# Attention over short heads, fused with two feed-forward layers and a second attention: a new order of halvings, row sums, reciprocal and quotient within a group, and one addition for both units of squares of 32

## The chip, the cores and the metric

The kernel runs on one core of one Trainium2 chip. The metric is the time of one execution on the device in microseconds (us), as the median of several runs. Besides that there is one execution that the hardware profiler recorded; every busy time, wait and start time below is from that one.

## The reference, cut to what matters

The input x has 8 batches of 512 tokens with 256 channels. Four layers are added to it one after the other: attention A, a feed-forward layer, attention B, and the same feed-forward layer again. The change touches attention A only. It does not attend over tokens. Each token is projected to 16 heads of 64 channels, and within one token and head every query channel attends to the key channels up to its own:

```python
scores = jnp.einsum('bshq,bshk->bshqk', Q, K)          # an outer product of 64 x 64 per token and head
mask = jnp.triu(jnp.ones((C, C), dtype=bool), 1)
scores = jnp.where(mask, -jnp.inf, scores)
w = jax.nn.softmax(scores, axis=-1)
attn = jnp.einsum('bshqk,bshk->bshq', w, V)
x = x + attn.reshape(b, s, HID) @ Wo + bo
```

So per token and head there is a lower triangle of 64 x 64 exponentials, its row sums (the denominators) and the row sums of exponentials times v (the numerators).

## The kernel before, in words

**Groups and units.** Attention A is cut into 128 groups: 8 batches, 4 groups of 4 heads each, 4 tiles of 128 tokens. In a group the 128 tokens lie on the partitions. The triangle of each head is cut into its diagonal and squares below it: one square of 32, two of 16, four of 8 and so on down to 32 of 1. The squares are worked off in four units, written here u0 to u3:

```python
units = (((32, 0, 2),), ((16, 0, 4),), ((32, 2, 2),), ((8, 0, 4), (4, 0, 4), (2, 0, 4), (1, 0, 4)))
```

Unit u0 has the squares of 32 of heads 0 and 1, u2 those of heads 2 and 3, u1 all squares of 16, u3 the small ones. A unit passes through these stages:

- `scores` (L784): products of queries and keys, by POOL for u0 and u2 in two halves and by DVE for u1 and u3. For u0 DVE also makes the diagonal (L771).
- `exps` (L798, L793): exponentials on ACT.
- `weigh` (L808, L805): exponentials times v on DVE, written beside the exponentials.
- `halve` (L814): for u0, u1 and u2, a DMA issued by POOL adds the second half of the tile onto the first (1 MB, an accumulating transfer).
- `fold` (L819): for u0 and u2, POOL adds two halves of what is left.
- `gather` (L845): row sums on DVE into small tiles `red`.
- `add_rows` (L852): POOL adds the tiles `red` to `acc`, which holds the denominators and numerators of the group.
- `small_squares` (L835, L852): POOL adds the squares of 2 and 1 of u3 to `acc` without a row sum.
- `invert` (L856), `divide` (L860): the reciprocal of the denominators on DVE, the quotient on POOL.
- `turn_group`, `project_out`, `new_x`: transposes and the output projection on PE, copies on ACT.

**Order.** The instructions of PE, DVE, ACT and POOL are issued in the order in which the program writes them down; only the loads on SP's queue are ordered by the build. `AttentionA.step(n)` writes one step of a software pipeline. Step n starts unit n (`scores`), makes the exponentials of unit n-1, weighs and halves unit n-2, and takes later stages of earlier units; `self.at(n - k)` is the unit of k steps ago. A step has three parts, ended by `yield`. Four steps make one group. After each part the main loop lets the generator `after_a` (feed-forward layers and attention B of the batches that attention A has done) write as much as a fixed pace allows; that starts at step 75. `later_weights` (`prep`) is a second generator that prepares weights for later layers and bounds for the scores at the start; one piece of it is written after every part from step 2 on. `fit_qkv(g)` fits the projection weights of head group g to the layer norm: g = 0 on DVE ahead of the loop, g = 1, 2, 3 on POOL after steps 0, 1, 2. `measure(b)` makes the layer-norm statistics of batch b ten steps ahead of its first unit.

**Buffers.** `w` (u0 and u2) has three buffers, `acc` three. Row sums of squares of 32 have two buffers `red64`, all others three buffers `red128`.

Of the kernel before, what the change touches and what calls it, by code (L numbers as in the profile page):

```python
# [9 lines left out]
F32 = mybir.dt.float32  # L10
# [3 lines left out]
ALU = mybir.AluOpType  # L14
AX = mybir.AxisListType

P = 128
# [9 lines left out]
GW = GH * C  # L27
NG = HID // GW
# [256 lines left out]
def fast_path(ctx: ExitStack, tc: tile.TileContext, k, t, flag):  # L285

    nc = tc.nc
# [123 lines left out]
    def later_weights():  # L411

        braw = block("braw")[0:3].rearrange("p (n f) -> p n f", n=4)
        part16 = block("part16", BF16)[0:3, : 2 * D]
        for j, row in enumerate((t.bo, t.b_bp)):
            nc.sync.dma_start(braw[:, 0, j * D : (j + 1) * D], row.broadcast_to([3, D]))
        yield
        for j in range(3):  # L420
            nc.scalar.copy(part16, braw[:, 0])
            nc.scalar.copy(braw[:, 2], part16)
            nc.gpsimd.tensor_tensor(braw[:, 0], braw[:, 0], braw[:, 2], ALU.subtract)
            yield
            if j == 0:
                nc.vector.tensor_scalar_mul(braw[:, 3], braw[:, 2], ident[0:3, 0:1])
            else:
                nc.vector.scalar_tensor_tensor(
                    braw[:, 3], braw[:, 2], ident[0:3, j : j + 1], braw[:, 3], ALU.mult, ALU.add
                )  # L430
        yield
        nc.scalar.copy(bias16.rearrange("p j f -> p (j f)"), braw[:, 3])

        wbqk = block("wbqk").rearrange("p (c f) -> p c f", c=DC)
        rows = block("rows")
        w3 = block("w3").rearrange("p (c f) -> p c f", c=MC)
        wbvp = block("wbvp")[:, : 2 * DC * D].rearrange("p (j c f) -> p j c f", j=2, c=DC)
        n_qk = 2 * BG * P
        s3 = rows[:, n_qk + D : n_qk + 2 * D]
        nc.sync.dma_start(s3, t.s3.broadcast_to([P, D]))  # L440
        nc.sync.dma_start(w3, t.w3.rearrange("(c p) f -> p c f", p=P))
        nc.sync.dma_start(wbqk, t.w_bqk.rearrange("(c p) j f -> p c (j f)", p=P))
        nc.sync.dma_start(wbvp[:, 0], t.w_bv.rearrange("(c p) f -> p c f", p=P))
        nc.sync.dma_start(wbvp[:, 1], t.w_bp.rearrange("(c p) f -> p c f", p=P))
        nc.sync.dma_start(
            rows[:, :n_qk], t.w_bqk[D - 1 : D].rearrange("o j f -> o (j f)").broadcast_to([P, n_qk])
        )
        nc.sync.dma_start(rows[:, n_qk : n_qk + D], t.w_bv[D - 1 : D].broadcast_to([P, D]))
        yield
        for c in range(MC):  # L450
            nc.gpsimd.tensor_tensor(w3[:, c, :], w3[:, c, :], s3, ALU.mult)
            if c % 2:
                yield
        for w, row, cols in ((wbqk, t.b_bqk_row, slice(0, n_qk)), (wbvp[:, 0], t.b_bv, slice(n_qk, n_qk + D))):
            for c in range(DC):
                nc.gpsimd.tensor_tensor(w[:, c], w[:, c], rows[:, cols], ALU.subtract)
                yield
            nc.sync.dma_start(w[P - 1 : P, DC - 1, :], row)

        nc.sync.dma_start(w3_d, w3.rearrange("p c f -> p (c f)"))  # L460
        nc.sync.dma_start(wbqk_d, wbqk.rearrange("p c f -> p (c f)"))
        nc.sync.dma_start(wbvp_d, wbvp.rearrange("p j c f -> p (j c f)"))
        yield
        yield from bound_scores()
# [139 lines left out]
    class AttentionA:  # L604
# [32 lines left out]

        def step(self, n):

            weighed = self.at(n - 2)  # L640
            if weighed[0] is not None:
                self.weigh(*weighed)
            unit = self.at(n)
            on_pool = unit[3] in (0, 2)
            if on_pool:
                half = self.scores(*unit)
                next(half)
            if weighed[0] is not None:
                self.halve(*weighed)
            if on_pool:  # L650
                next(half, None)
            b, i, g, u = self.at(n + 40)
            if u == 0 and g == 0 and i == 0 and b > 0:
                self.x[b] = load_x(b)
            b, i, g, u = self.at(n + 10)
            if u == 0 and g == 0 and i == 0:
                self.measure(b)
            b, i, g, u = self.at(n + 8)
            if u == 0 and g == 0:
                self.live["xn"] = normed(self.x[b][:, i, :], *self.rn[b, i], "a")  # L660
            b, i, g, u = self.at(n - 5)
            if u == NU - 1:
                self.invert(b, i, g)
            b, i, g, u = self.at(n - 4)
            if u == 1:
                self.gather(b, i, g, u)
            b, i, g, u = self.at(n + 7)
            if u == 0 and g == 0:
                nc.scalar.copy(self.live[b, i], self.live.pop("ps_ln"))
            if self.at(n - 1)[0] is not None:  # L670
                self.exps(*self.at(n - 1))
            yield
            if unit[0] is not None and not on_pool:
                for _ in self.scores(*unit):
                    pass
            for args in self.sums:
                self.add_rows(*args)
            self.sums = []
            b, i, g, u = self.at(n - 5)
            if u == NU - 1:  # L680
                self.divide(b, i, g)
            b, i, g, u = self.at(n - 2)
            if u == NU - 1:
                self.small_squares(b, i, g)

            b, i, g, u = self.at(n - 4)
            if u == 0:
                self.fold(b, i, g, u)
            b, i, g, u = self.at(n - 3)
            if u == 2:  # L690
                self.fold(b, i, g, u)
            b, i, g, u = self.at(n - 9)
            if u == NU - 1:
                self.new_x(b, i, g)
            b, i, g, u = self.at(n + 2)
            if u == 0:
                self.keep_qk(b, i, g)
            b, i, g, u = self.at(n - 7)
            if u == NU - 1:
                self.turn_group(b, i, g)  # L700
            b, i, g, u = self.at(n - 8)
            if u == NU - 1:
                self.project_out(b, i, g)
            b, i, g, u = self.at(n + 3)
            if u == 0:
                self.project(b, i, g)
            yield
            b, i, g, u = self.at(n - 4)
            if u == 2:
                self.gather(b, i, g, u)  # L710
            b, i, g, u = self.at(n - 5)
            if u == 0:
                self.gather(b, i, g, u)
            b, i, g, u = self.at(n - 3)
            if u == NU - 1:
                self.gather(b, i, g, u)
            b, i, g, u = self.at(n - 7)
            if u == NU - 1:
                nc.scalar.copy(self.live["att"], self.live.pop("pta"))
            b, i, g, u = self.at(n + 8)  # L720
            if u == 0 and g == 0:
                self.live[b, i] = lnp.tile([P, DC, P], F32, tag="xnt_a", name=f"xnta_{b}_{i}", bufs=NT)
                self.live["ps_ln"] = turned_over(self.live.pop("xn"), half_bank().rearrange("p (c s) -> p c s", c=DC))
            yield
# [113 lines left out]
        def gather(self, b, i, g, n_u):  # L838


            w = self.live.pop((b, i, g, n_u))
            for n, off, nsq, cols in squares(units[n_u]):
                if n > 2:
                    red = ap_.tile([P, 2, nsq * n], F32, tag=f"red{nsq * n}", name=f"red_{b}_{i}_{g}_{n_u}_{n}", bufs=2 + (n < 32))
                    nc.vector.tensor_reduce(red, self.columns_of(w, n, off, nsq), AX.X, ALU.add)  # L845
                    self.sums.append((b, i, g, n, cols, red))

        def add_rows(self, b, i, g, n, cols, part):

# [491 lines left out]
    with tc.manual_schedule(engines={ET.PE, ET.DVE, ET.Activation, ET.Pool}):  # L1341
        a = AttentionA()
        prep = later_weights()
        fit_qkv(0)
        weights = None
        done, spent = after_a(), 0
        for n in range(-10, a.steps):
            for part, _ in enumerate(a.step(n)):
                if n >= 2:
                    next(prep, None)  # L1350
                while 3 * spent * each < total * (3 * (n - each - 11) + part + 1):
                    spent += next(done)
            if 0 <= n < NG - 1:
                fit_qkv(n + 1)
        for _ in done:
            pass
    judge()
# [86 lines left out]
```

## Time and profile before

| | |
|---|---|
| median of 3 runs | 4010.42 us (4006.96 to 4017.54) |
| the profiled execution | 4009.55 us, span 4007.6 us |
| PE busy | 2958.0 us (74%) |
| DVE busy | 3376.7 us (84%) |
| ACT busy | 2337.2 us (58%) |
| POOL busy | 3098.1 us (77%) |
| transfers of q0, POOL's queue | 570.46 MB, 62.9% of 16 engines' span |
| granted TensorE clock, mean | 0.845 |

The span runs from the first to the last instruction; the profiled execution takes 2 us more. Four stretches differ in kind. Up to about 200 us the pipeline fills and weights are prepared. From 201 to 509 us attention A runs alone, 13 groups. From 580 to 3653 us feed-forward layers and attention B of earlier batches are woven in, 107 groups. From 3653 us on only the last batch's later layers are left, and PE is busy for 322 of 355 us. In a group of rows "busy, mean ns" is the time of the whole group and of one instruction; consecutive instructions of one engine overlap by up to 0.1 us, or by up to 0.3 us on POOL, so a chain is summed from start to next start. A DMA on POOL's queue holds POOL for some 0.6 us and lands later.

### The profile page before, as it was taken

Reading aid. Unit: us, or ns where it says so; the run is one execution under the profiler, and the core shown is the slowest. Engines: PE = TensorE matmul, PEld = TensorE weight load, DVE = VectorE, ACT = ScalarE, POOL = GpSimd, SP = SyncE. Lnnn points to the kernel's source line nnn. Section 1 sums busy time; section 2 is a strip of 40 time slices with the busy share of each in tenths; the row PEclk is TensorE's granted clock in tenths of the full one; section 3 lists DMA queues with packets and bytes.
Section 4 is the critical chain, followed back from the end, with each engine's and each line's share of the span. In section 5 each row is a group of like instructions: output and inputs, shape, how many; then the busy total and the mean of one; then the engine's idle time right before and its main releaser. Section 6 shows DMA issues by size and latency. Waiting matters only on the chain.

```text
span 4007.6 us, 37678 instructions
## 1 busy us (share of the span) xinstructions
PE 2958.0 (74%) x12328; PEld 2012.2 (50%) x12328; DVE 3376.7 (84%) x3777; ACT 2337.2 (58%) x3145; POOL 3098.1 (77%) x3051
## 2 busy tenths in 40 slices
PE   1543478777876888768787788768787778768988
PEld 0311145355653656346553566346653556436847
DVE  4899988998889888998989988998889988897115
ACT  2433465666755766666755767567656667555342
POOL 6688888887888887887888888888888878886211
PEclk7555689888987989889897889879898899879999
DMA  8566777668776777668776688668877687767304
GB/s 240 114 141 145 146 182 182 147 161 199 199 162 126 195 188 196 150 147 210 174 192 139 168 198 214 147 131 198 195 181 151 154 199 205 155 133 210 126 29 167
DMA packets 118653, 671.07 MB, mean 167 GB/s; under 512 B 12704, under 2 KB 31915, under 8 KB 43824
## 3 DMA queue, kind: packets, MB, share of 16 engines
q0 software_dynamic: 78336, 570.46, 62.9%
q1 hardware_dynamic: 40112, 98.11, 6.8%
q8 instruction: 100, 1.64, 0.2%
q14 instruction: 105, 0.86, 0.1%
HBM read 255.90 MB, written 9.96 MB: 66 GB/s over the span
## 4 chain that ended last, share of the span: by engine, by line
DVE 38%; PE 16%; POOL 14%; DMA 12%; issue 8%; ACT 8%; POOLq 0%; DVEq 0%; ACTq 0%
DVE red L845 15%; DMA w<-w 12%; DVE w L808 10%; PE ph L1120 5%; ACT w L798 3%; POOL w L819 3%; DVE ws L808 3%; POOL w L784 3%; PE pqkb L1167 3%; DVE ws L784 3%; POOL acc L852 3%; DVE w L784 2%; POOL w L814 2%; DVE acc L856 2%; POOL h L1036 2%
## 5 line engine op out<-in xcount | busy, mean ns | idle before, releaser
L798 ACT ACTIVATE w<-w 128x2048 f32<-128x2048 f32 x384 | 734.2, 1913 | 653.8 <-POOL w L784 440.8
L1120 PE MATMUL ph<-h,hidden 128*128 128x512 f32 x4096 | 1047.9, 412 | 77.4 <-POOL h L1036 45.5
L784 POOL TENSOR_TENSOR w<-k 128x1024 f32<-128x1024 f32 x512 | 1076.2, 2102 | 9.6 <-ACT k L762 9.0
L1120 PEld LDWEIGHTS ph<-h,hidden 128*128 128x128 f32 x4096 | 795.3, 196 | 282.1 <-POOL h L1036 55.9
L808 DVE TENSOR_TENSOR w<-w,qv 128x1024 f32<-128x1024 f32 x768 | 899.8, 1213 | 22.4 <-ACT w L798 22.3
L845 DVE TENSOR_REDUCE red<-w 128x128 f32<-128x1024 f32 (+1 forms) x384 | 601.8, 1567 | 171.6 <-DMA w<-w 94.6
L819 POOL TENSOR_TENSOR w<-w 128x1024 f32<-128x1024 f32 x256 | 643.1, 2512 | 72.5 <-DMA w<-w 71.9
L814 POOL DMA_DIRECT2D w<-w x384 | 337.1, 878 | 339.7 <-issue 134.8
L852 POOL TENSOR_TENSOR acc<-acc,red 128x256 f32<-128x256 f32 (+1 forms) x640 | 471.0, 736 | 152.3 <-DVE red L845 124.5
L845 DVE TENSOR_REDUCE red<-ws 128x256 f32<-128x2048 f32 (+1 forms) x256 | 435.5, 1743 | 0.0
L746 PE MATMUL qv<-wqv,xnta 128*128 128x512 f32 x512 | 299.3, 715 | 89.9 <-DVE ws L808 82.4
L808 DVE TENSOR_TENSOR ws<-ws,qv 128x1024 f32<-128x1024 f32 (+3 forms) x512 | 294.7, 638 | 49.4 <-ACT ws L798 49.4
L1052 PE MATMUL pw<-xnt,gate 128*128 128x512 f32 (+2 forms) x1152 | 298.8, 419 | 24.9 <-ACT silu L1028 18.0
L784 DVE TENSOR_TENSOR w<-qv,k 128x1024 f32<-128x1024 f32 x256 | 301.3, 1219 | 3.6
L784 DVE TENSOR_TENSOR ws<-qv,k 128x1024 f32<-128x1024 f32 (+3 forms) x512 | 299.8, 648 | 0.0
L868 PE MATMUL bank<-ident,acc 128*128 128x128 f32 x256 | 64.3, 341 | 287.5 <-ACT k L761 287.1
L798 ACT ACTIVATE ws<-ws 128x1920 f32<-128x1920 f32 x128 | 231.5, 1809 | 75.3 <-DVE ws L784 74.7
L1052 PEld LDWEIGHTS pw<-xnt,gate 128*128 128x128 f32 x1152 | 227.6, 213 | 82.1 <-ACT silu L1028 22.3
L1229 ACT ACTIVATE eb<-psb 128x256 f32<-128x256 f32 (+3 forms) x512 | 182.2, 443 | 146.6 <-PE psb L1226 146.3
L1146 PE MATMUL pof<-w,h 128*128 128x256 f32 x1024 | 247.9, 396 | 19.4 <-ACT h L1085 19.4
L1085 ACT ACTIVATE h<-ph,s_sb 128x512 fp32r<-128x512 f32 (+1 forms) x256 | 171.1, 688 | 145.9 <-PE ph L1120 144.6
L856 DVE RECIPROCAL acc<-acc 128x256 f32<-128x256 f32 x128 | 223.2, 1744 | 12.3 <-POOL acc L852 12.3
(143 smaller groups left out, 4723.5 us busy)
## 6 DMA issues: line engine op xcount, KB each, us to landing
w<-w POOLq DMA_DIRECT2D x384, 1024.0 KB, 7.7
hidden<-in_h POOLq DMA_DIRECT2D x128, 1024.0 KB, 7.9
gate<-in_w12p POOLq DMA_DIRECT2D x32, 1024.0 KB, 9.0
w<-w_d SPq DMA_DIRECT2D x16, 1024.0 KB, 12.0
wqv<-wqv_d SPq DMA_DIRECT2D x31, 512.0 KB
wo<-in_wo SPq DMA_DIRECT2D x32, 256.0 KB, 7.4
wbqk<-wbqk_d SPq DMA_DIRECT2D x8, 1024.0 KB
w<-in_h SPq DMA_DIRECT2D x8, 1024.0 KB, 7.0
```

The lines of the kernel that those rows point to most:

```text
L746: nc.tensor.matmul(qv.rearrange("p j f -> p (j f)"), xnt[:, c, :], wqv[:, c, :], start=(c == 0), stop=(c == DC - 1),)
L784: eng.tensor_tensor(e, rows(q).to_broadcast(shape), columns(kt[:, 0]).to_broadcast(shape), ALU.mult)
L798: nc.scalar.activation(e, e, AF.Exp, scale=C**-0.5)
L808: nc.vector.tensor_tensor(ev, e, columns(qv[:, 1]).to_broadcast(list(e.shape)), ALU.mult)
L814: nc.gpsimd.dma_start(w[:, :2048], w[:, 2048:], accum_op=ALU.add)
L819: nc.gpsimd.tensor_tensor(w[:, :1024], w[:, :1024], w[:, 1024:2048], ALU.add)
L845: nc.vector.tensor_reduce(red, self.columns_of(w, n, off, nsq), AX.X, ALU.add)
L852: nc.gpsimd.tensor_tensor(rows, rows, part.rearrange("p a (x i) -> p a x i", i=n), ALU.add)
L856: nc.vector.reciprocal(acc[:, 0, :], acc[:, 0, :])
L1052: nc.tensor.matmul(pj[:, toks], w[:, m % 4, j, c, :], xs[:, p, c, toks], start=(p == 0 and c == 0), stop=(p == 1 and c == DC - 1),)
L1120: nc.tensor.matmul(pss[j], w[:, j, c, :], h_in(p, c), start=(p == 0 and c == 0), stop=(p == 1 and c == MC - 1),)
L1146: nc.tensor.matmul(po, h(0, c)[:, i * P : (i + 1) * P], w3[:, c, :], start=(c == 0), stop=False)
```

## The change

- The fold of u0 moves from step n-4, second part, to step n-3, first part, ahead of POOL's scores and of the halving of u1.
- The row sum of u1 stays in its step but moves ahead of `weigh`. The row sum of u0 moves from n-5 to n-4, that of u2 from n-4 to n-5, both in the third part. The row sums of u3 stay.
- The reciprocal moves from n-5 to n-6, to the very start of the step; the quotient from n-5 to n-6, second part, behind the fold of u2.
- The row sums of u0 and u2 go into the two halves of one tile `red1`, and one addition per group takes both. All other row sums use `red0`. Both have two buffers.
- `measure(0)` is written ahead of `fit_qkv(0)`. `prep` advances once a step, from step 3 on. `fit_qkv(1)`, `(2)`, `(3)` come after steps 4, 14 and 24.

```diff
         def step(self, n):
+            b, i, g, u = self.at(n - 6)
+            if u == NU - 1:
+                self.invert(b, i, g)
+            b, i, g, u = self.at(n - 4)
+            if u == 1:
+                self.gather(b, i, g, u)
             weighed = self.at(n - 2)
             if weighed[0] is not None:
                 self.weigh(*weighed)
+            b, i, g, u = self.at(n - 3)
+            if u == 0:
+                self.fold(b, i, g, u)
             unit = self.at(n)
...
             if u == 0 and g == 0 and i == 0:
-                self.measure(b)
+                if b > 0:
+                    self.measure(b)
...
-            b, i, g, u = self.at(n - 5)
-            if u == NU - 1:
-                self.invert(b, i, g)
-            b, i, g, u = self.at(n - 4)
-            if u == 1:
-                self.gather(b, i, g, u)
...
             self.sums = []
-            b, i, g, u = self.at(n - 5)
-            if u == NU - 1:
-                self.divide(b, i, g)
             b, i, g, u = self.at(n - 2)
             if u == NU - 1:
                 self.small_squares(b, i, g)
 
-            b, i, g, u = self.at(n - 4)
-            if u == 0:
-                self.fold(b, i, g, u)
             b, i, g, u = self.at(n - 3)
             if u == 2:
                 self.fold(b, i, g, u)
+            b, i, g, u = self.at(n - 6)
+            if u == NU - 1:
+                self.divide(b, i, g)
...
             yield
             b, i, g, u = self.at(n - 4)
-            if u == 2:
+            if u == 0:
                 self.gather(b, i, g, u)
             b, i, g, u = self.at(n - 5)
-            if u == 0:
+            if u == 2:
                 self.gather(b, i, g, u)
...
                 if n > 2:
-                    red = ap_.tile([P, 2, nsq * n], F32, tag=f"red{nsq * n}", name=f"red_{b}_{i}_{g}_{n_u}_{n}", bufs=2 + (n < 32))
-                    nc.vector.tensor_reduce(red, self.columns_of(w, n, off, nsq), AX.X, ALU.add)
-                    self.sums.append((b, i, g, n, cols, red))
+                    if n_u != 2:
+                        self.live["red", n] = ap_.tile(
+                            [P, 2, GW // 2], F32, tag=f"red{n // 32}", name=f"red{n}_{b}_{i}_{g}"
+                        )
+                    red = self.live["red", n]
+                    part = red[:, :, cols.start // 2 : cols.stop // 2]
+                    nc.vector.tensor_reduce(part, self.columns_of(w, n, off, nsq), AX.X, ALU.add)
+                    if n_u != 0:
+                        self.sums.append((b, i, g, n, slice(0, GW), red))
...
         a = AttentionA()
         prep = later_weights()
+        a.measure(0)
         fit_qkv(0)
...
-                if n >= 2:
+                if n >= 3 and part == 2:
                     next(prep, None)
...
-            if 0 <= n < NG - 1:
-                fit_qkv(n + 1)
+            if n in (4, 14, 24):
+                fit_qkv(n // 10 + 1)
```

## The prediction

> **What bounds the kernel now.** I began with the busy time by stretch, because the shares of the whole span mix three stages. Attention A alone runs from 201 to 509 us, attention A with the feed-forward work woven in from 580 to 3653 us, and the last batch's remainder from there to the end.
>
> ```profile
> 201.00:509.00 308.00, 124.20 (x215) 58.67 (x215) 307.42 (x319) 119.97 (x122) 269.00 (x238) 0.55 0.70 146
> 580.00:3653.00 3073.00, 2393.12 (x10211) 1635.39 (x10210) 2768.40 (x3107) 1975.45 (x2653) 2558.38 (x2512) 0.87 0.74 173
> ```
>
> The columns are PE, PEld, DVE, ACT, POOL. In the first stretch DVE is busy 307.42 of 308 us: it is the bound and waits for nothing. The reciprocal runs once a group and 13 times there, so a group costs 308/13 = 23.7 us. In the second it runs 107 times: 3073/107 = 28.7 us a group, with DVE busy 25.9 and POOL 23.9. DVE has 2.8 us of gaps in each group. The waits of DVE there, then the landing of the halvings (L814) in the two stretches:
>
> ```profile
> DVE red L845 <- DMA w<-w: 84.0, 37, 4.9
> DVE red L845 <- POOL w L819: 72.2, 27, 5.6
> DVE acc L856 <- POOL acc L852: 11.4, 10, 2.2
> ```
> ```profile
> DMA to landing us min/median/max: 6.9/7.1/8.0
> ```
> ```profile
> DMA to landing us min/median/max: 6.9/7.8/16.7
> ```
>
> So 156 us are lost ahead of row sums. No halving ever lands in less than 6.9 us. Last, the timeline of one group without feed-forward work, DVE and then POOL:
>
> ```profile
> 331.17 1.74 DVE L856 RECIPROCAL acc<-acc 128x256 f32<-128x256 f32 x1
> 332.83 2.28 DVE L808 TENSOR_TENSOR ws<-ws,qv 128x1024 f32<-128x1024 f32 x4
> 335.03 2.28 DVE L845 TENSOR_REDUCE red<-w 128x256 f32<-128x2048 f32 x1
> 337.34 2.36 DVE L784 TENSOR_TENSOR w<-qv,k 128x1024 f32<-128x1024 f32 x2
> ```
> ```profile
> 326.93 0.87 POOL L814 DMA_DIRECT2D w<-w  x1 [2.65 <-issue]
> 327.54 2.35 POOL L852 TENSOR_TENSOR acc<-acc,red 128x128 f32<-128x128 f32 x3
> 329.86 1.95 POOL L784 TENSOR_TENSOR w<-k 128x1024 f32<-128x1024 f32 x1
> 331.75 0.85 POOL L814 DMA_DIRECT2D w<-w  x1
> 332.36 2.23 POOL L784 TENSOR_TENSOR w<-k 128x1024 f32<-128x1024 f32 x1
> 334.28 0.98 POOL L860 TENSOR_TENSOR acc<-acc 128x256 f32<-128x256 f32 x1
> 334.96 2.60 POOL L819 TENSOR_TENSOR w<-w 128x1024 f32<-128x1024 f32 x1
> 337.45 0.79 POOL L852 TENSOR_TENSOR acc<-acc,red 128x256 f32<-128x256 f32 x1
> 338.14 0.67 POOL L835 TENSOR_TENSOR ws<-ws 128x256 f32<-128x256 f32 x1
> 338.89 1.66 POOL L852 TENSOR_TENSOR acc<-acc,ws 128x256 f32<-128x256 f32 x2
> 340.50 2.36 POOL L819 TENSOR_TENSOR w<-w 128x1024 f32<-128x1024 f32 x1
> 342.83 1.96 POOL L784 TENSOR_TENSOR w<-k 128x1024 f32<-128x1024 f32 x1
> 344.73 0.85 POOL L814 DMA_DIRECT2D w<-w  x1
> ```
>
> Both engines keep the program's order. What matters is distance: before, several other instructions stand between each halving and its reader, and between the last sums (327.54) and the small squares (338.14).
>
> **What the Trainium skill says.** "DMA: Bandwidth & Descriptors", section SWDGE vs HWDGE vs iDMA: an accumulating transfer can be issued from GpSimd only. The trace agrees, all 384 stand in POOL's queue, so each waits behind what POOL was given earlier. The same page, Anatomy of one DMA: a transfer's semaphore wait happens on the issuing sequencer before dispatch; and its fit, 2.0 us plus bytes over 436 thousand, gives an estimate of 4.4 us for 1 MB. The trace differs, 6.9 at the least, and decides. "Trainium Architecture — The Big Picture", Inside one NeuronCore: engines run in parallel and meet only at semaphores. The trace agrees: the 2.65 us of POOL at 326.93 end with DVE's product.
>
> **The change part by part.** I number a group's steps r0 to r3 (step n modulo 4) and its units u0 to u3. After the change POOL's order is: r0 scores of u0 (first half), halving of u2, scores of u0 (second half), *one* addition for both squares of 32; r1 addition of 16, small squares, fold of u2, quotient; r2 scores of u2 (first half), halving of u0, second half; r3 fold of u0, halving of u1, two additions. DVE in r1 is: reciprocal, row sum of u1, products of u3, scores of u1.
>
> Two new waits come of it. First, the fold of u0 stood in r0 behind three other steps' work and now follows its halving with only half a score between (1.92 us): POOL must wait for the landing, and the halving of u1 is queued behind that wait. Second, u2's row sum moves to the end of r3, so the addition of 32 comes after r0's scores on POOL; the reciprocal is DVE's very next work and waits for it, and behind the reciprocal are queued the row sum of u1 and the products of u3, for which POOL's small squares wait. POOL waits for DVE and DVE for POOL, in turn.
>
> This closes a chain that comes back to its own start one group later. From start to next start in the timeline above: reciprocal 1.66, row sum of u1 2.31, products of u3 2.28 (together 6.25 on DVE); small squares with their additions 2.36, fold of u2 2.33, quotient 0.69, half a score 1.90 (7.28 on POOL); landing of u0 at the least 6.9 and its hand-over 0.07 (6.97); fold of u0 2.37, issue of u1's halving 0.61, two additions 1.39, half a score 1.90, issue of u2's halving 0.61, half a score 1.92, addition of 32 0.73 (9.53); hand-overs 0.1. The sum is 30.1 us, against 23.7. The same method on the order of before (row sum of u1, addition, small squares, fold, scores, addition, halving of u1, landing) gives 19.8, under DVE's 23.7, as the full DVE shows.
>
> With feed-forward work: the median landing is 0.7 longer (7.8 for 7.1). POOL's feed-forward work between 580 and 3653 us (L1036 144, L934 102, L529 to L532 107) is 353/107 = 3.3 us a group; of twelve places where it is put, six lie on the chain (the others fall into POOL's two waits): 1.65. I add 0.5 for late landings of u2 and waits of that work: 33.0 us a group, 4.3 more than 28.7. Bounds: 30.5, if all of it hides and landings are short; 34.5, if it all lies on the chain.
>
> The rest is small. One addition fewer a group saves 128 x 0.69 = 88 us of POOL's time, counted in the chain already. Moving batch 0's statistics ahead of fitting g = 0: the row sum of x waits until 14.65 us behind the fit, though x is there at 3; the projection still needs the fitted weights, so I take 3 us of 22 (bounds 0 and 7). Preparation once a step and the three later fits: before, ACT stood 21.9 us for the load of `sk` and DVE 24.7 behind it; groups 0 to 5 took 165 us (36 to 201). After: 5 x 30.1 plus half of the preparation's 16 us of POOL (L423 4.3, L451 5.5, L456 6.6; half of its places are on the chain), 159. Its SP loads now have two steps to land; I keep 5 us for what stays (0 to 15). The fits lie in POOL's waits: nothing, 11 us at most if that cover is gone. Together about -4. One buffer fewer for `red` costs nothing: POOL has read each before its turn to be filled comes again. The end after 3653 is bound by PE (322 of 355 us busy): unchanged.
>
> Sum: -4 + 13 x 6.4 (83) + 107 x 4.3 (460) = +539. The two groups between 509 and 580 are left equal. On the profiled execution's 4009.55 us (span 4007.6, 2 around it; the median of the runs, 4010.42, is 1 away) that is **4550 us**.
>
> **The rivals.** *Only the transfers bind*: the reciprocal finds its sums ready, for instance because POOL runs ahead. The chain is then row sum 2.31, products 2.28, POOL 7.28, landing 6.97, fold 2.37, landing of u1 6.9: 28.1 alone; with two landings longer by 0.7, two of twelve places (0.55) and the 0.5 above, 30.6: 13 x 4.4 + 107 x 1.9 - 4 = +256, 4266 us. For it speaks that today's reciprocal waits only 11.4 us in all; against it, that the addition is now later than the scores in POOL's order.
>
> *Faster*: DVE stays the bound, and the 156 us ahead of row sums go, since folds and sums of u2 stand a step further apart, and some 25 us at the start: about 3830 if all, 3900 if half the former comes back as other waits. It decides from the point where the chain is under 28.7 us a group. My sum is above it by 4.3, and by 1.4 even alone with the shortest landings; a mis-read order of one queue would be needed.
>
> *The change doesn't do what it says*: the order is not kept by the engines, and the time is 4010. The trace of before shows the written order on both, so this is small.
>
> **How the numbers follow.** Main case 0.72, transfers only 0.19, faster 0.06, no change 0.03. The main case alone reaches from 4250 (30.5 us a group) to 4660 (34.5); the second lies inside. So 4250 to 4650 leaves out the 0.09 of the other two and the ends. About 0.3%, 12 us, is what a measurement of this kernel can tell from no change. Slower 0.92, same 0.02, faster 0.06.
>
> **What would show it.** Right: groups of about 30 us before the feed-forward starts, DVE busy there near 78% and no longer full; the reciprocal waiting some 5 us for POOL's addition in most groups; POOL's fold waiting some 4 us for the landing of u0; the halving of u1 issued over 9 us after that of u0, where it was 5.9 (from 321.02 to 326.93). Wrong: a group still at 23.7 us in that stretch, or a reciprocal that doesn't wait (then the second case), or row sums of u1 that wait for the transfer.

## The result and the profile after

The median of 4 runs is 4628.45 us (4626.05 to 4630.83), against 4008.69 us (4004.39 to 4017.54) for the kernel before on the same chip: 1.1543 times as long, with a 95% interval from 1.1521 to 1.1564. The profiled execution took 4626.84 us, its span is 4625.0 us. That is 617 us more than the profiled execution before. First the engines' busy time over the whole span, and its share of the span:

```profile
PE 3042.5 (66%) x12328; PEld 2037.5 (44%) x12328; DVE 3381.9 (73%) x3777; ACT 2341.9 (51%) x3145; POOL 3074.4 (66%) x2923
```

DVE is busy for 3381.9 us, as before (3376.7), but that is now 73% of the span where it was 84%. The same two stretches as in the prediction show where the rest went. The columns are again PE, PEld, DVE, ACT, POOL, and then the granted TensorE clock, the busy share of the DMA engines and their GB/s; 13 reciprocals, so 13 groups, fall in the first stretch and 107 in the second:

```profile
193.00:592.00 399.00, 140.86 (x314) 78.13 (x313) 314.14 (x328) 124.90 (x129) 273.75 (x228) 0.53 0.55 114
672.00:4262.00 3590.00, 2475.56 (x10218) 1658.59 (x10216) 2768.94 (x3107) 1980.86 (x2655) 2537.86 (x2404) 0.83 0.64 148
```

Alone, a group takes 399/13 = 30.7 us (23.7 before) and DVE is busy 79% of it; it is no longer the bound. With feed-forward work it takes 3590/107 = 33.55 us (28.7 before). DVE's work in 107 groups is what it was (2768.94 us, 2768.40 before), so all that was added there is idle time. Over the whole span, the waits at three places before, and then DVE's and POOL's main waits after, are these; an entry gives the waiting engine and line, what it waited for, the total in us, how often, and the longest:

```profile
DVE acc L856 <- POOL acc L852: 12.3, 11, 2.2
DVE red L845 <- DMA w<-w: 94.6, 39, 7.2
POOL w L819 <- DMA w<-w: 71.9, 23, 6.1
```

```profile
DVE acc L863 <- POOL acc L859: 683.4, 121, 10.5
DVE red L851 <- POOL w L820: 69.8, 41, 4.4
DVE red L851 <- DMA w<-w: 8.5, 3, 5.9
```
```profile
POOL acc L859 <- DVE red L851: 478.4, 126, 5.4
POOL w L820 <- DMA w<-w: 435.7, 113, 6.7
POOL ws L836 <- DVE ws L809: 171.3, 126, 1.7
```

The reciprocal (L863), which waited 12.3 us in all before, waits for POOL's addition in 121 of 128 groups. The row sums of u1 hardly wait for a transfer any more: 94.6 us became 8.5. POOL waits in turn for DVE's row sum and small products and for landings. Within the stretch with feed-forward work, the reciprocal's wait is

```profile
DVE acc L863 <- POOL acc L859: 565.3, 100, 10.5
```

against the 11.4 us that the prediction shows for this stretch before. That is more than the 517 us by which the stretch grew, so little room is left for another cause there, such as the granted TensorE clock, which fell from 0.87 to 0.83. The landing of the halvings (L815), in the stretch alone and then in the one with feed-forward work:

```profile
DMA to landing us min/median/max: 6.9/7.6/8.9
```
```profile
DMA to landing us min/median/max: 6.9/7.8/16.0
```

The shortest is unchanged, and with feed-forward work so is the median. Alone the median rose from 7.1 to 7.6 us, but only the halvings of u2 became longer (7.33 to 7.85), and their fold comes 12 us later; those of u0 and u1 stay at 6.9 and 7.0. What changed is who stands waiting for them. The chain that ended last, as shares of the span by engine, names POOL where it named DVE before; before, then after:

```profile
DVE 38%; PE 16%; POOL 14%; DMA 12%; issue 8%; ACT 8%; POOLq 0%; DVEq 0%; ACTq 0%
```
```profile
POOL 42%; DVE 22%; issue 17%; PE 13%; ACT 3%; DMA 3%; POOLq 0%; SPq 0%; DVEq 0%; ACTq 0%
```

One whole turn of the loop can be read off the timeline of a group alone. The columns are start, duration, engine, line, operation, tiles and, in brackets, the idle time ahead of it with its releaser. DVE from one reciprocal to the next, then POOL:

```profile
459.06 1.75 DVE L863 RECIPROCAL acc<-acc 128x256 f32<-128x256 f32 x1 [5.40 <-POOL acc L859]
460.73 2.23 DVE L851 TENSOR_REDUCE red<-w 128x256 f32<-128x2048 f32 x1
462.88 2.33 DVE L809 TENSOR_TENSOR ws<-ws,qv 128x1024 f32<-128x1024 f32 x4
...
489.53 1.75 DVE L863 RECIPROCAL acc<-acc 128x256 f32<-128x256 f32 x1 [6.54 <-POOL acc L859]
```
```profile
463.10 0.73 POOL L859 TENSOR_TENSOR acc<-acc,red 128x256 f32<-128x256 f32 x1 [4.08 <-DVE red L851]
465.15 0.61 POOL L836 TENSOR_TENSOR ws<-ws 128x256 f32<-128x256 f32 x1 [1.32 <-DVE ws L809]
465.85 1.66 POOL L859 TENSOR_TENSOR acc<-acc,ws 128x256 f32<-128x256 f32 x2
467.46 2.37 POOL L820 TENSOR_TENSOR w<-w 128x1024 f32<-128x1024 f32 x1
469.78 0.73 POOL L867 TENSOR_TENSOR acc<-acc 128x256 f32<-128x256 f32 x1
470.47 1.96 POOL L785 TENSOR_TENSOR w<-k 128x1024 f32<-128x1024 f32 x1
472.37 0.84 POOL L815 DMA_DIRECT2D w<-w  x1
472.98 2.23 POOL L785 TENSOR_TENSOR w<-k 128x1024 f32<-128x1024 f32 x1
479.38 2.36 POOL L820 TENSOR_TENSOR w<-w 128x1024 f32<-128x1024 f32 x1 [4.17 <-DMA w<-w]
481.68 0.86 POOL L815 DMA_DIRECT2D w<-w  x1
482.29 1.82 POOL L859 TENSOR_TENSOR acc<-acc,red 128x256 f32<-128x256 f32 x2
484.06 1.95 POOL L785 TENSOR_TENSOR w<-k 128x1024 f32<-128x1024 f32 x1
485.95 0.88 POOL L815 DMA_DIRECT2D w<-w  x1
486.56 2.26 POOL L785 TENSOR_TENSOR w<-k 128x1024 f32<-128x1024 f32 x1
488.48 1.01 POOL L859 TENSOR_TENSOR acc<-acc,red 128x256 f32<-128x256 f32 x1
```

Follow it once round. The reciprocal at 459.06 waited 5.40 us; row sum and products of u3 follow it directly, POOL's small squares wait for those products (465.15), then POOL works without a gap to the halving of u0 at 472.37. Its fold stands only half a score later and waits 4.17 us. Behind it are queued the halving of u1 (481.68, 9.31 us after that of u0), the scores of u0 and the addition at 488.48, and 489.53 is the next reciprocal: 489.53 - 459.06 = 30.47 us.

### The profile page after: what moved, and what is told of

Same layout as the page of the kernel before. It is cut to its first block, busy times and chain, and to the rows that moved or that the text cites. A ratio compares the mean times of both kernels' runs of the same rounds, so it can differ in the third digit from the quotient of the medians.

```text
span 4625.0 us, 38060 instructions
## 1 busy us (share of the span) xinstructions
PE 3042.5 (66%) x12328; PEld 2037.5 (44%) x12328; DVE 3381.9 (73%) x3777; ACT 2341.9 (51%) x3145; POOL 3074.4 (66%) x2923
## 4 chain that ended last, share of the span: by engine, by line
POOL 42%; DVE 22%; issue 17%; PE 13%; ACT 3%; DMA 3%; POOLq 0%; SPq 0%; DVEq 0%; ACTq 0%
POOL w L785 15%; POOL w L820 9%; DVE red L851 8%; POOL acc L859 6%; POOL w L815 5%; DVE ws L809 5%; PE ph L1127 4%; DVE w L809 3%; DMA w<-w 2%; POOL h L1043 2%; PE pw L1059 2%; DVE w L785 2%; PE qv L747 2%; PE pof L1153 2%; ACT w L799 1%
## 5 line engine op out<-in xcount | busy, mean ns | idle before, releaser
L747 PE MATMUL qv<-wqv,xnta 128*128 128x512 f32 x512 | 443.9, 1018 | 990.5 <-DVE ws L809 870.4
L820 POOL TENSOR_TENSOR w<-w 128x1024 f32<-128x1024 f32 x256 | 608.5, 2377 | 505.9 <-DMA w<-w 435.7
L859 POOL TENSOR_TENSOR acc<-acc,red 128x256 f32<-128x256 f32 x512 | 441.5, 862 | 492.6 <-DVE red L851 478.4
L863 DVE RECIPROCAL acc<-acc 128x256 f32<-128x256 f32 x128 | 224.3, 1753 | 683.4 <-POOL acc L859 683.4
L747 PEld LDWEIGHTS qv<-wqv,xnta 128*128 128x128 f32 x512 | 140.9, 303 | 1166.0 <-issue 696.2
L815 POOL DMA_DIRECT2D w<-w x384 | 337.4, 879 | 28.4 <-DVE acc L772 16.4
L799 ACT ACTIVATE ws<-ws 128x1920 f32<-128x1920 f32 x128 | 231.8, 1811 | 28.1 <-DVE ws L785 27.6
L1153 PE MATMUL pof<-w,h 128*128 128x256 f32 x1024 | 235.0, 383 | 0.0
```

The lines of the kernel that those rows point to most:

```text
L747: nc.tensor.matmul(qv.rearrange("p j f -> p (j f)"), xnt[:, c, :], wqv[:, c, :], start=(c == 0), stop=(c == DC - 1),)
L799: nc.scalar.activation(e, e, AF.Exp, scale=C**-0.5)
L815: nc.gpsimd.dma_start(w[:, :2048], w[:, 2048:], accum_op=ALU.add)
L820: nc.gpsimd.tensor_tensor(w[:, :1024], w[:, :1024], w[:, 1024:2048], ALU.add)
L859: nc.gpsimd.tensor_tensor(rows, rows, part.rearrange("p a (x i) -> p a x i", i=n), ALU.add)
L863: nc.vector.reciprocal(acc[:, 0, :], acc[:, 0, :])
```

## The experiments

"Alone" and "with feed-forward" are us per group in the two kinds of stretch, the first as the median over the groups from one end of u0's products to the next, the second as the mean. Before: 23.72 and 28.72. After: 30.45 and 33.55. Ratios are to the kernel before, with the 95% interval.

**The parts that only remove work: start, joined sums, both.** Each is put alone into the kernel before.

```diff
 # start: measure(0) ahead of fit_qkv(0), and
-                if n >= 2:
+                if n >= 3 and part == 2:
                     next(prep, None)
-            if 0 <= n < NG - 1:
-                fit_qkv(n + 1)
+            if n in (4, 14, 24):
+                fit_qkv(n // 10 + 1)
 # joined: the change's edit of gather() and nothing else
```

> The kernel before with only the edits at the start (statistics of batch 0 first, preparation once a step, fits after steps 4, 14 and 24). Theory (two waits in one chain make the loss; the start is a gain): the first groups come sooner, group 5 some 20 to 35 us earlier, nothing else moves: 3975 to 3990 us, 0.5 to 0.9% faster. Rival (the start edits carry part of the loss, because fits and preparation now stand between the scores for longer): 4010 us or more.

> The kernel before with only the joined row sums of both units of squares of 32 (one addition a group in place of two, four buffers for row sums in place of five). Theory: no part of the loss; POOL does 0.7 us less a group where DVE is the bound, so 3980 to 4012 us, within 0.3% or a little faster. Rival (fewer buffers or the later joined addition make the loss): well above 4100 us, with row sums that wait for POOL's additions.

> The kernel before with the edits at the start and the joined row sums, all else as it was. Theory: the two gains measured apart (0.38% and 0.35%) add, since one lies in the first five groups and the other in later ones: 3980 us, 3974 to 3990. Rival (both gains come from the same slack): 3994 us or more.

Start: 3995.25 us, 0.9962 [0.9948, 0.9976]. Group 5 ended the products of u0 at 171.7 us where it was 201.1, 29 us sooner, as expected. But some 9 us were given back in the groups after it (24.54 us mean alone, 23.89 before): the last of the preparation on DVE (L389 to L402, 5.4 us) and one wait of 3.0 us now fall there. So the total lies above the range expected. Joined: 3999.55 us, 0.9965 [0.9951, 0.9979]; 23.72 alone and 28.62 with feed-forward. Both: 3978.21 us, 0.9916 [0.99, 0.9933]; the gains add. Neither is part of the loss, so the order within a group has to carry all of it.

**The fold of u0 alone, in the old order.**

```diff
 # on the kernel before
             if weighed[0] is not None:
                 self.weigh(*weighed)
+            b, i, g, u = self.at(n - 3)
+            if u == 0:
+                self.fold(b, i, g, u)
...
-            b, i, g, u = self.at(n - 4)
-            if u == 0:
-                self.fold(b, i, g, u)
```

> The kernel before with the fold of u0 alone moved ahead of u1's halving. Theory (the chain sums): row sum of u1, addition, small squares, fold of u2, half a score, landing of u0, fold of u0, landing of u1 close a chain of 26.3 us, 2.6 more than DVE's 23.7, without any late reciprocal; POOL's fold waits some 4 us for the landing in most groups. With feed-forward work about 30: 4180 us, 4120 to 4250. Rival (the fold's wait costs only together with the late reciprocal): 4010 us.

4219.24 us, 1.0517 [1.0495, 1.0539]; 26.24 alone, 30.39 with feed-forward, as expected. The waits of this kernel, then one of its folds in POOL's timeline:

```profile
POOL w L819 <- DMA w<-w: 464.0, 142, 7.3
DVE acc L856 <- POOL acc L852: 231.8, 102, 6.5
```
```profile
443.86 2.36 POOL L819 TENSOR_TENSOR w<-w 128x1024 f32<-128x1024 f32 x1 [3.77 <-DMA w<-w]
```

One moved instruction makes POOL wait for the landing (72 us of such waits before, 464.0 now). The reciprocal, which was not touched, begins to wait as well: the addition that it needs is issued by POOL behind that fold.

**Both waits undone, the rest of the new order left.** The later reciprocal at the step's start, u1's row sum ahead of u3's products, the joined sums and the new start stay.

```diff
 # on the kernel after
-            b, i, g, u = self.at(n - 3)
-            if u == 0:
-                self.fold(b, i, g, u)
             unit = self.at(n)
...
+            b, i, g, u = self.at(n - 4)
+            if u == 0:
+                self.fold(b, i, g, u)
             b, i, g, u = self.at(n - 3)
             if u == 2:
                 self.fold(b, i, g, u)
...
-            b, i, g, u = self.at(n - 4)
+            b, i, g, u = self.at(n - 5)
             if u == 0:
                 self.gather(b, i, g, u)
-            b, i, g, u = self.at(n - 5)
+            b, i, g, u = self.at(n - 4)
             if u == 2:
                 self.gather(b, i, g, u)
```

> The changed kernel with the fold and row sum of u0 and the row sum of u2 all put back; what stays of the new order is the reciprocal at the start of its step, a step later, and the row sum of u1 ahead of u3's products, besides joined sums and the start. Theory: both waits are gone, the reciprocal waits for almost nothing. But u1's row sum now stands only 6.5 us of DVE's work after u1's products (8.7 before), less than a landing of 6.9 us, so it waits about 0.6 us in each group without feed-forward work (24.3 us a group) and about 1 us more than before with it: 4020 to 4180 us, likeliest 4100. Rival (the place of u1's row sum is free, all the loss lay in the two waits): 3980 to 3995 us, as the start and the joined sums alone give.

4096.21 us, 1.022 [1.0201, 1.024]; 24.86 alone, 29.50 with feed-forward. The total is as expected. What is left of the loss is seen in DVE's wait (94.6 us before) and its timeline:

```profile
DVE red L851 <- DMA w<-w: 222.8, 87, 6.3
```
```profile
442.13 2.29 DVE L851 TENSOR_REDUCE red<-w 128x256 f32<-128x2048 f32 x1 [1.12 <-DMA w<-w]
```

It is u1's row sum, which now stands ahead of u3's products and waits for its landing: 24.86 - 23.72 = 1.14 us a group, where 0.6 was expected. The halving is issued 0.53 us after u1's products end (434.49, 435.02), and the expectation counted the landing from that end. So undoing the two waits named in the prediction brings back 30.45 - 24.86 = 5.6 of the 6.7 us lost alone. The next experiments take them one at a time.

**Only the late addition left: the fold of u0 back.** The edit above without its last four lines: fold and row sum of u0 go back, u2's row sum stays late.

> The changed kernel with the fold and the row sum of u0 put back where they were, so that the fold is no longer ahead of u1's halving; the late addition of 32 ahead of the reciprocal stays. Theory (chain of two waits): the chain loses landing and fold of u0, 9.3 us, gains 2.5 us of POOL that they covered, and is 23.9 us alone, about DVE's own 23.7; with feed-forward work some 29.5 us a group: 4050 to 4150 us. Rival (the loss lies in the reciprocal's wait alone): above 4400 us. Rival (neither wait, something else in the change): 4600 us.

4311.71 us, 1.0746 [1.0726, 1.0765]; 27.47 alone, 31.17 with feed-forward. This missed. DVE's timeline and then POOL's around one reciprocal tell why:

```profile
441.72 0.42 DVE L772 TENSOR_TENSOR acc<-qv,k 128x256 f32<-128x256 f32 x1
445.93 1.75 DVE L863 RECIPROCAL acc<-acc 128x256 f32<-128x256 f32 x1 [3.79 <-POOL acc L859]
```
```profile
442.35 0.88 POOL L815 DMA_DIRECT2D w<-w  x1 [0.70 <-DVE acc L772]
442.96 2.26 POOL L785 TENSOR_TENSOR w<-k 128x1024 f32<-128x1024 f32 x1
444.87 1.02 POOL L859 TENSOR_TENSOR acc<-acc,red 128x256 f32<-128x256 f32 x1
```

The expectation summed POOL's legs and the landings, and left out the loop that runs through DVE's own work. DVE ends its step with the products of u2 and u0's diagonal (441.72) and comes to the reciprocal at once. But POOL's halving of u2 has been waiting for those products. (The view names the diagonal, which is DVE's last work before it; the products ended at 441.80, and the halving starts 0.55 us later, as it does behind products elsewhere.) Half a score and the addition follow. So DVE does its 23.7 us of work and then stands for POOL's 3.8: 27.5, which is what was measured.

**Only the landing loop left: the addition early.** There are two ways: u2's row sum goes back to n-4, or, with that row sum left late, the addition moves ahead of u0's scores on POOL.

```diff
 # first: on the kernel after
-            b, i, g, u = self.at(n - 5)
+            b, i, g, u = self.at(n - 4)
             if u == 2:
                 self.gather(b, i, g, u)
 # second: on the kernel after, at the very start of step()
+            if self.at(n - 6)[3] == 2:
+                for args in self.sums:
+                    self.add_rows(*args)
+                self.sums = []
```

> The changed kernel with only the row sum of u2 put back to its old step, so that the addition of 32 is made before POOL's scores and the reciprocal finds it ready; the early fold of u0 stays. Theory (chain of two waits): the chain now closes over the landing of u1: 28.1 us a group alone, 30.6 with feed-forward work, 4270 us, 4230 to 4330. The reciprocal waits for little, the row sum of u1 waits for the transfer in most groups. Rival (the reciprocal's wait alone makes the loss): 4000 us. Rival (something else): 4600 us.

> The changed kernel with one edit: the addition of the squares of 32 ahead of POOL's scores of u0. Theory (two waits, each with its own chain): the reciprocal's wait goes and the chain over the landing of u1 stays, as when u2's row sum was put back: 28.1 us a group alone, some 31.7 with feed-forward work, 4380 us, 4340 to 4420. Rival (the reciprocal needs u2's row sum back in its old step): 4600 us.

First: 4389.41 us, 1.0939 [1.0919, 1.0959]; 28.10 alone, 31.73 with feed-forward. Second: 4370.65 us, 1.0895 [1.0838, 1.0953]; 28.09 and 31.51. The rival "only the transfers bind" had its sum at 28.1 alone, and that is what remains once the reciprocal's leg is cut, by either edit. With feed-forward the sum (30.6) was 0.9 to 1.1 too short; the waits of the first of the two say where the time is, here DVE's and then POOL's:

```profile
DVE red L851 <- DMA w<-w: 231.1, 93, 7.1
DVE acc L863 <- POOL acc L859: 151.5, 80, 4.6
```
```profile
POOL w L820 <- DMA w<-w: 538.4, 149, 6.2
```

POOL's folds and DVE's row sum of u1 wait for landings, as that rival has it. But in 80 groups the reciprocal waits too, which that rival's sum leaves out; by which of POOL's work the addition is late there was not taken apart. The second edit also shows that not the row sum's step was wrong but the addition's place behind u0's scores.

**The fold behind the halving of u1.** The fold of u0 moves to the second part of its step, behind u1's halving and the two additions, and is still ahead of u0's scores.

```diff
 # on the kernel after
-            b, i, g, u = self.at(n - 3)
-            if u == 0:
-                self.fold(b, i, g, u)
             unit = self.at(n)
...
-            if u == 2:
+            if u in (0, 2):
                 self.fold(b, i, g, u)
```

> The changed kernel with one edit: the fold of u0 in the second part of its step, behind u1's halving and the two additions. Theory (chain with DVE's own work in it, which my sum for the run with the fold put back had left out): from the reciprocal to the end of u1's products DVE needs 16.6 us, from there POOL 10.1 us (halving 0.6, two additions 1.8, fold 2.3, half a score 1.9, halving 0.6, half a score 1.9, addition 1.0) to the next reciprocal: 26.7 us a group alone, some 30.4 with feed-forward work: 4220 us, 4180 to 4290. Rival (the sum without DVE's part, 23.9): 4000 us.

4427.19 us, 1.1036 [1.0985, 1.1088]; 28.14 alone, 32.06 with feed-forward. This missed too. POOL's timeline of one group:

```profile
447.05 0.84 POOL L812 DMA_DIRECT2D w<-w  x1
...
454.12 2.36 POOL L817 TENSOR_TENSOR w<-w 128x1024 f32<-128x1024 f32 x1 [0.84 <-DMA w<-w]
456.42 1.96 POOL L782 TENSOR_TENSOR w<-k 128x1024 f32<-128x1024 f32 x1
...
460.84 1.01 POOL L856 TENSOR_TENSOR acc<-acc,red 128x256 f32<-128x256 f32 x1
```

The halving at 447.05 is that of u0. POOL's wait has shrunk from 4.17 to 0.84 us, which looks like a cure, but the fold still starts 7.07 us after its halving and u0's scores and the addition still follow the fold. Only what moved into the gap left the loop: the issue of u1's halving and the two additions, 2.38 us by the table below, and 30.45 - 2.38 = 28.07, where 28.14 was measured. A wait that shrinks because other work fills it gives back that work's time here, and no more.

**A version with the same moves that gains.** The reciprocal and u1's row sum stand behind u3's products, the small squares ahead of the additions, the fold of u2 a step later, and the fold of u0 behind u1's halving in the second part. Then, on top, the addition of 32 ahead of u0's scores, and last u0's fold and row sum back in their old steps.

```diff
 # first, on the kernel after: invert (n - 6) and gather of u1 (n - 4) stand
 # behind weigh and the scores of POOL instead of ahead of them; and
-            for args in self.sums:
-                self.add_rows(*args)
-            self.sums = []
             b, i, g, u = self.at(n - 2)
             if u == NU - 1:
                 self.small_squares(b, i, g)
-            b, i, g, u = self.at(n - 3)
-            if u == 2:
-                self.fold(b, i, g, u)
+            for args in self.sums:
+                self.add_rows(*args)
+            self.sums = []
             b, i, g, u = self.at(n - 6)
             if u == NU - 1:
                 self.divide(b, i, g)
+            b, i, g, u = self.at(n - 4)
+            if u == 2:
+                self.fold(b, i, g, u)
+            b, i, g, u = self.at(n - 3)
+            if u == 0:
+                self.fold(b, i, g, u)
 # second, on the first: the early addition shown above
 # third, on the second:
-            b, i, g, u = self.at(n - 3)
+            b, i, g, u = self.at(n - 4)
             if u == 0:
                 self.fold(b, i, g, u)
...
-            b, i, g, u = self.at(n - 4)
+            b, i, g, u = self.at(n - 5)
             if u == 0:
                 self.gather(b, i, g, u)
```

> The changed kernel with its folds, reciprocal and additions written where their inputs are long there: reciprocal and row sum of u1 behind u3's products, small squares ahead of the additions, the fold of u2 a step later (behind u2's scores and u0's halving), the fold of u0 behind u1's halving and the two additions. Row sums of u0 and u2, joined sums and the start stay as changed. Theory: no halving is queued behind a landing, the reciprocal comes 3.7 us of DVE's work after u2's products where POOL needs 3.5 to make the addition, u1's row sum 11 us after its products, u2's folds 15 us after the halving. DVE is full again without feed-forward work (23.7 us a group) and near its own 26.5 with it: 3830 to 3920 us, faster than both kernels. Rival (row sums of u0 and u2 in their new places, or the later reciprocal, cost by themselves): above 4010 us.

> The kernel of the spread order, with one thing more: the addition of the squares of 32 stands ahead of POOL's scores of u0, not behind them. In the spread order the reciprocal still waited 1.3 us for it (25.1 us a group without feed-forward work in place of 23.7). Theory (the reciprocal's wait is a matter of what stands ahead of the addition in POOL's order): the wait goes, 23.7 to 24.0 us a group alone, about 28.0 with feed-forward work: 3890 to 3960 us. Rival (the later row sum of u2 costs by itself, or POOL then waits for it): the addition waits for DVE, the group stays at 25 us, above 4040 us.

> The same with the fold and row sum of u0 back in their old steps, behind POOL's scores, so that POOL reaches the scores of u0 and the halving of u2 2.3 us sooner. Theory: without feed-forward work no change from the run beside it (DVE full either way); with it the halving of u2 is no longer late: 3880 to 3960 us. Rival (buffers: the scores of u2 then wait for u0's row sum, as in the kernel before): slower than the run beside it by 20 us or more.

First: 4079.15 us, 1.0166 [1.0149, 1.0183]; 25.13 alone, where 23.7 was expected. POOL's addition of 32 and then DVE's reciprocal:

```profile
422.78 0.99 POOL L859 TENSOR_TENSOR acc<-acc,red 128x256 f32<-128x256 f32 x1
```
```profile
423.81 1.75 DVE L863 RECIPROCAL acc<-acc 128x256 f32<-128x256 f32 x1 [1.31 <-POOL acc L859]
```

DVE comes to the reciprocal 1.3 us before the addition is done. POOL works without a gap for 9.5 us up to that addition, and in this stretch stands the fold of u0 (2.3 us), which the old order had behind the scores; no run takes it out of this kernel alone. The second kernel moves only the addition: **3949.06 us, 0.985 [0.9834, 0.9867]**, faster than both kernels. Its two stretches, again with 13 and 107 groups, and one addition and the reciprocal that needs it:

```profile
176.00:488.00 312.00, 139.33 (x304) 76.70 (x304) 311.06 (x325) 122.45 (x126) 272.62 (x227) 0.57 0.70 146
...
556.00:3587.00 3031.00, 2376.83 (x10214) 1634.20 (x10213) 2767.83 (x3107) 1983.57 (x2656) 2545.58 (x2405) 0.88 0.75 176
```
```profile
406.72 0.72 POOL L863 TENSOR_TENSOR acc<-acc,red 128x256 f32<-128x256 f32 x1
```
```profile
410.77 1.75 DVE L867 RECIPROCAL acc<-acc 128x256 f32<-128x256 f32 x1
```

The addition ends at 407.44, 3.3 us before DVE comes to the reciprocal. DVE is full again alone (311.06 of 312 us), and 3031/107 = 28.33 us with feed-forward is 0.4 less than before. The third kernel took 3955.42 us, 0.9859 [0.9842, 0.9875]: u0's earlier fold and row sum bring nothing that can be measured here. POOL waits 140.3 us there for row sums ahead of its scores, as the rival has it, and that costs nothing that can be measured either. Of the 1.5%, start and joined sums alone make 0.84%.

## Why the prediction was right

The loop of two waits was the right mechanism: 4550 us were predicted and 4628 measured. Times of the profiled execution, stretch by stretch:

| stretch | predicted | measured |
|---|---|---|
| up to group 5 | -4 | 193.6 - 201.1 = -7.5 |
| 13 groups alone | 13 x 6.4 = +83 | 398.9 - 310.5 = +88 |
| the two groups between | 0 | 80.1 - 68.4 = +11.7 |
| 107 groups with feed-forward | 107 x 4.3 = +460 | 3590 - 3073 = +517 |
| the end | 0 | 362.0 - 354.5 = +7.5 |
| sum | +539 | +617 |

The legs of the loop (medians alone; means with feed-forward in the last column), each from start to next start:

| leg | predicted alone | measured alone | measured with feed-forward |
|---|---|---|---|
| reciprocal, row sum u1, products u3 | 6.25 | 6.09 | 6.09 |
| small squares, fold u2, quotient, half a score | 7.28 | 7.21 | 7.89 |
| landing of u0 and hand-over | 6.97 | 7.01 | 8.01 |
| fold u0 to halving u1 | 2.37 | 2.30 | 2.33 |
| halving u1 and two additions | 2.00 | 2.38 | 3.42 |
| half a score, halving u2 | 2.51 | 2.51 | 2.72 |
| half a score, addition of 32 | 2.65 | 2.95 | 3.10 |
| sum (predicted with hand-overs 0.1) | 30.1 | 30.45 | 33.6 |

- **The loop alone.** 30.1 for 30.45. Two terms were short: the pair of additions (1.77 us rather than 1.39) and the last leg, each by 0.3 to 0.4; the legs of DVE, of the small squares and of the fold were together 0.3 long. The landing of u0 was 6.94 at the median, the least value seen before, as assumed.
- **The loop with feed-forward.** The supplement was 2.85 and came out at 33.55 - 30.7 = 2.9. The longer landing (0.7 predicted, 7.69 - 6.94 = 0.75 measured) and the POOL work and late landings put on the chain were together sized well; their shares were not measured apart. The base under them, 30.7 as the mean alone, is 0.6 above the 30.1 predicted. That is the +57 us by which this row exceeds its prediction.
- **The two groups between and the end.** They were left equal. The two groups lengthened by 5.9 us each, like their neighbours: leaving them out was a wrong step, by 12 us. The cause of the last 7.5 us stays open; PE is busy for 2.6 us more there.
- **The start.** The first products of u0 end 36.2 - 32.5 = 3.7 us sooner (3 predicted), though 0.8 of that is an earlier start of the fit, whose weights landed sooner (12.91 to 12.14). Groups 0 to 5 took 161 us (165 before; 159 predicted, and 5 kept for what stays, of which 2 came). The start's edits in the old order give 139 us for the same groups, so the edits did their work and the new order took most of it back at once.
- **What was to be seen.** DVE busy 79% alone (78 predicted); the reciprocal waits 683.4/128 = 5.3 us a group (5); POOL's fold waits 4.16 us alone at the median (4); u1's halving comes 9.3 us after u0's (over 9). All four hold, and row sums of u1 wait for a transfer in only 3 cases, as the main case has it.
- **The range.** Its ends are not the sums of the bounds they are named with: 30.5 and 34.5 us a group, put into the prediction's own sum, give 4281 and 4709 us, where 4250 and 4660 are stated. The measured time lies 22 us under the 4650 given as the upper end.
- **The rivals.** "Only the transfers bind" has its 28.1 us alone, but as the next loop underneath: it shows when the addition is made early. "Faster" asked for a chain under 28.7 us; it is what the early addition and the spread order reach with the same late row sum of u2. "Doesn't do what it says" is excluded by the timeline.
- **How the loss divides alone.** u1's row sum ahead of u3's products 1.1 us; with it, the late addition makes 3.8 (27.47), the landing loop 4.4 (28.1), both together 6.7 (30.45). They do not add up, because they are not parts of one sum: the time of a group follows the longest loop, and each kernel has another one.

## What to carry to other kernels

In a software pipeline on queues that keep their order, sum every loop that comes back to its own start a group later, through each engine and each landing, including the one that runs through the busiest engine's whole work; here the longest, once found, gave the time of a group alone to within 0.4 us. The expectations that missed a time alone had left out one leg or a whole loop. Before moving an instruction, look at what is queued behind it and at how far its input's producer stands away: in the spread order, one addition ahead of two half scores or behind them decided between 1.5% faster and 1.7% slower.

## What was not expected of the hardware

- A halving lands in 6.94 us at the median in the stretch alone for u0, with only half a score running on POOL meanwhile and DMA engines busy 55% of the time. In the kernel before it was the same 6.94 with DMA engines busy 70%: more calm does not bring it nearer to the estimate of 4.4 us from the fit in the Trainium skill, "DMA: Bandwidth & Descriptors", Anatomy of one DMA. No run here shows why.
- On POOL, an addition of 128x128 took 701 ns (L852 before), one of 128x256 behind a fold 0.73 us, a fold of 128x1024 2.37 us: a quarter of the elements costs a third, an eighth hardly less (their layouts differ). The joined sums take one addition of 701 ns from each group, 89.7 us in all; the busy time of these additions fell by 48.8 us (179.4 + 291.6 before, 422.2 with joined sums alone), so the joined ones are not as cheap as the rows of narrow ones suggest. The sum of the prediction had 88 us here, without weight in its result.
- An addition or fold directly behind the second half of the scores is recorded 0.3 us longer than elsewhere (1.01 against 0.73, in the spread order 2.64 against 2.36), its start lying 0.3 us inside the record before it (486.56 + 2.26 = 488.82, where the addition starts at 488.48). A chain on POOL is therefore summed from start to next start, and the record's length is not used.
- A halving that waits for DVE's products starts 0.55 us after they end. In the kernel before, POOL stands idle ahead of 173 halvings; 139 of them start 0.50 to 0.60 us after the end of DVE's last products, though the view names ACT, the diagonal or "issue" for many of these waits (so for the 2.65 us ahead of 326.93 in the prediction, where the products end at 326.40). A fold that waits for a landing starts 0.07 us after it, and a reciprocal that waits for POOL 0.03 us. A loop with a waiting halving in it is longer by this hand-over, which no expectation here had counted.
